# A six-stage decoder on one core: the last batch's front is laid beside the attentions

## The chip, the cores and the metric

The kernel runs on one core of one Trainium2 chip. A core has a matrix engine (TensorE, PE in the profile; the loading of its weights is shown apart as PEld), a vector engine (DVE), a scalar engine (ACT), a general engine that here issues gathers (POOL), and a queue engine that issues plain transfers (SP). Every engine takes its instructions strictly in the order of its own list, and waits at an instruction until the semaphores that it names have been raised by other engines or by transfers. The metric is the device time of one execution in microseconds (us), as the median of several runs.

## The reference

The input is `x` of 4 batches x 256 tokens x 256 channels, in float32. Six residual stages follow one another; each reads the layer-normalised sum so far:

```python
x = x + attn0(ln(x))      # gated linear attention: 16 heads, a decaying scan over the 256 tokens of a batch
x = x + experts4(ln(x))   # 4 experts chosen by token id; weights are the context itself
x = x + peer(ln(x))       # 8 heads x 8 of 2025 experts per token: gather 64 rows, weigh, add
x = x + local(ln(x))      # causal convolution (3 taps), 8-head attention within blocks of 16 tokens, projection
x = x + cross(ln(x), ctx) # 16-head attention of all 1024 tokens to all 1024 context rows, with int8-like rounding
x = x + moe(ln(x))        # top 2 of 16 experts, and a shared one
```

Three of them matter in detail. The denominator of the linear attention is one number per token and head:

```python
running_kv, running_ksum = scan(k * v, decay), scan(k, decay)
den = clip(sum(q * running_ksum, -1, keepdims=True), 1e-6)
out = (q * running_kv / den) @ w_out
```

The gathered experts of the third stage:

```python
z = einsum('btd,bthkd->bthk', h, down_embed[indices])     # 64 rows of 128 per token
z = silu(z * softmax(scores))
out = einsum('bthk,bthkd->btd', z, up_embed[indices])     # 64 rows of 256 per token
```

And the cross attention, where every query head sees all 1024 keys, so that a softmax row has 1024 elements:

```python
q, k, v = fake_quantised(x @ Wq + bq), fake_quantised(ctx @ Wk + bk), fake_quantised(ctx @ Wv + bv)
attn = softmax(q @ k.T); attn = round(attn / (max / 255)) * (max / 255)
out = (attn @ v) @ Wp + bp
```

## The kernel before

The 1024 tokens are eight tiles of 128 tokens (`xt[0]` to `xt[7]`, kept in SBUF throughout), two for each of four batches. Batch b has tiles 2b and 2b+1.

**Streams and the planner.** Everything up to the mixture of experts is written as Python generators, called streams. While the program is built, `Clock.weave` (L110) advances at each step the stream that can go on earliest by a rough clock. `Clock.note` (L80) prices each instruction, and a `yield` names the engine that comes next and, if need be, a condition. The order in which instructions are recorded becomes the fixed order of PE, ACT and DVE. Nothing is reordered on the chip: an instruction that is recorded early and not ready holds up all that stands behind it on its engine. Nearly all instructions are recorded through one helper, so that they carry line L76 in the profile and are told apart by their tiles.

**The fronts** (`front`, L348). A front is the first three stages up to the choice of the gathered experts for one batch (two tiles): normalisation, projections, scans, division by the denominator, four context experts, up and down projection, similarities, and top-k by MAX8 and FIND_INDEX8. Its outcome is `idxT[t]` and `pT[t]`, the row numbers and weights of a tile; from then on tile t is `known`. `follow` (L1122) starts front 2 when tile 1 is known and front 3 when tile 3 is known. The fronts use seven PSUM banks as one set of slots (`bank`, L346). An eighth bank, `accs`, holds the sums of the gathers and of the cross attention.

**The gathers** (`fetches`, L607, and `weigh`, L618). Each tile has eight chunks, 64 in all. For a chunk, SP issues two broadcast loads (`hb`), and POOL issues eight indirect gathers into one of three `g` buffers. DVE multiplies and reduces (`g`, `z`, `u`), ACT takes a tanh (`th`), DVE writes weights into `blk`, and PE adds eight matmuls into `accs`. The fetch of chunk n waits until chunk n-3 has been summed. After a tile's eighth chunk DVE adds `accs` to `xt[t]`; the tile is then `added`.

**The hand-over** (`turn`, L748). When all four fronts and the keys and values are done, the fronts' memory and banks are given up at once, the weights of the later stages are loaded into that memory, and PSUM is divided anew: two double banks `sc` for scores, one bank `tp`, two banks `mm`.

**Local attention, queries and units.** `locals_` (L940) takes the groups (0,1), (2,3), (4,5), (6), (7) one after another, each once its tiles are added. `local_attention` (L806) normalises, convolves, projects, attends within blocks, adds to `xt`, and then in the same generator normalises again, forms and rounds the queries and transposes them into `qT`. `units` (L947) are three streams that share 128 units, 16 heads for each of eight tiles. A unit is: two score matmuls into an `sc` slot, a maximum over 1024 scores (DVE), `nb` (DVE), an exponential to 8-bit `e` (ACT), two transposes into `tp` (PE), a cast `qqT` (ACT), and eight small matmuls into `accs`. After the 16th unit of a tile `cross_out` (L987) divides (`ao`) and projects; then `route` (L1032) normalises, chooses two of 16 experts and adds the shared one.

**The end.** Once tile 7 is added, the gathers' memory is given up and `weights` (L792) loads the experts' `w13`. After the last `route` the slots are worked out, and 31 tiles of routed rows run through `up` (L1200) and `down` (L1221); the results are gathered and written out.

Of the kernel before, what the change touches and what calls it, by code (L numbers as in the profile page):

```python
# [11 lines left out]
F32 = mybir.dt.float32  # L12
# [39 lines left out]
class Clock:  # L52
# [6 lines left out]
    def __init__(self, nc):  # L59
        self.free = dict.fromkeys(("tensor", "scalar", "vector", "gpsimd", "sync"), 0.0)  # L60
        self.t = self.end = 0.0
        self.last = None
        for name in self.free:
            setattr(self, name, self._Engine(self, name, getattr(nc, name)))
# [15 lines left out]
    def note(self, engine, op, out, args, kw):  # L80
        if engine == "sync":
            return
        n, late = math.prod(out.shape[1:]), 0.0
# [5 lines left out]
        elif engine == "scalar":  # L89
            scaled, summed = isinstance(kw.get("scale"), bass.AP), "accum_out" in kw  # L90
            cost, late = 0.06 + n * 0.00083 + 0.23 * (scaled or summed) + 0.06 * (scaled and summed), 0.1
        elif engine == "gpsimd":
            cost = 1.23
        elif op in ("max", "max_index", "tensor_reduce"):
            src = args[1] if op != "max_index" else args[2]
            cost = (0.195 if op == "tensor_reduce" else 0.16) + 0.00104 * math.prod(src.shape[1:])
        elif op == "reciprocal":
            cost = 0.1 + 0.0064 * n
        elif op == "tensor_tensor_scan":
            cost = 0.2 + 0.0022 * n  # L100
        else:
            cost = 0.195 + (0.00054 if op in ("tensor_scalar", "tensor_copy") else 0.00104) * n
        if self.last not in (None, engine):
            self.t = self.end + self.HOP
        start = max(self.free[engine], self.t)
        self.free[engine] = start + cost
        self.end = max(self.end, start + cost + late)
        self.last = engine

    def weave(self, streams):  # L110

# [3 lines left out]
        while live:  # L115
            able = []
            for s in live:
                t = s.t
                engine, wait = s.wait
                if isinstance(wait, Slots):  # L120
                    if not wait.left:
                        continue
                    t = max(t, wait.at)
                elif wait is not None:
                    at = wait()
                    if at is None:
                        continue
                    t = max(t, at)
                able.append((max(t, self.free[engine]), t, s))
            _, t, s = min(able, key=lambda x: (x[0] - x[2].lead, x[1]))  # L130
            self.lead = s.lead
# [7 lines left out]
            s.t = self.end + self.HOP  # L139

    def fork(self, *gens):

        made = [Stream(g, self.lead, self.end + self.HOP) for g in gens]
# [4 lines left out]
class Stream:  # L148
    def __init__(self, gen, lead=0.0, start=0.0):
        self.gen, self.lead, self.t, self.done = gen, lead, start, None  # L150
# [3 lines left out]
class Slots:  # L154
# [3 lines left out]
    def __init__(self, clock, pool, tag, n):  # L158
        self.clock, self.pool, self.tag, self.left, self.at = clock, pool, tag, n, 0.0
        self.n = n  # L160

    def take(self, shape, dtype=F32):
        while not self.left:
            yield "tensor", self
        self.left -= 1
        return self.pool.tile(shape, dtype, name=self.tag, tag=self.tag, bufs=self.n)

    def give(self):
        self.left += 1
        self.at = self.clock.end  # L170


def decoder(ctx, tc, a, out):
# [7 lines left out]
    front_ctx = ctx.enter_context(ExitStack())  # L181
    attend_ctx = ctx.enter_context(ExitStack())
    work_ctx = ctx.enter_context(ExitStack())
    A = SimpleNamespace(turned=None)
    wa = front_ctx.enter_context(tc.tile_pool(name="wa", bufs=1, side="right"))

# [29 lines left out]
    wkv = load(wa, "wkv", [P, 2, 2 * D], rows("wkv"))  # L216
    bk_b = load(wa, "bkb", [P, D], a["bkv"][:, 0:D].to_broadcast([P, D]))
    bv_c = load(base, "bv_c", [P, 2])
    for b in range(2, NB):
# [11 lines left out]
    headones = wa.tile([P, P // XD, XD], F32, name="headones", tag="headones")  # L231
    nc.gpsimd.memset(headones, 1.0)
    nc.gpsimd.affine_select(out=headones, in_=headones, compare_op=ALU.is_ge, fill=0.0, base=0,
                            pattern=[[-XD, P // XD], [0, XD]], channel_multiplier=1)
    nc.gpsimd.affine_select(out=headones, in_=headones, compare_op=ALU.is_ge, fill=0.0, base=XD - 1,
                            pattern=[[XD, P // XD], [0, XD]], channel_multiplier=-1)
# [28 lines left out]

    gather_ctx = ctx.enter_context(ExitStack())
    gather = gather_ctx.enter_context(tc.tile_pool(name="gather", bufs=3))
    fr = front_ctx.enter_context(tc.tile_pool(name="fr", bufs=1, side="right"))
    psum_ctx = ctx.enter_context(ExitStack())
    psp = psum_ctx.enter_context(tc.tile_pool(name="psp", bufs=1, space=PSUM))  # L270
    psf = front_ctx.enter_context(tc.tile_pool(name="psf", bufs=1, space=PSUM))
# [13 lines left out]
    def layernorm_T(pool, sfx, bank, tiles, dst, col0=0, store=None):  # L285
# [3 lines left out]
        for i, t in enumerate(tiles):  # L289
            st = pool.tile([P, 6], F32, name="ln_st", tag="ln_st" + sfx, bufs=2)  # L290
            ve_.bn_stats(st, xt[t])
            ve_.bn_aggr(mv[:, i, :], st)

        ve = pool.tile([P, n], F32, name="ln_ve", tag="ln_ve" + sfx)
        ve_.tensor_scalar(ve, mv[:, :, 1], EPS, None, ALU.add)
        half = pool.tile([P, n], I32, name="ln_half", tag="ln_half" + sfx)
        ve_.tensor_scalar(half, ve.bitcast(I32), 1, None, ALU.logical_shift_right)
        rstd = pool.tile([P, n], F32, name="ln_rstd", tag="ln_rstd" + sfx)
        ve_.tensor_scalar(rstd.bitcast(I32), half, -1.0, float(0x5F3759DF), ALU.mult, ALU.add)
        nt = pool.tile([P, n], F32, name="ln_nt", tag="ln_nt" + sfx)  # L300
        for _ in range(3):
            ve_.scalar_tensor_tensor(nt, rstd, -0.5, rstd, ALU.mult, ALU.mult)
            ve_.tensor_tensor(nt, nt, ve, ALU.mult)
            ve_.scalar_tensor_tensor(rstd, nt, 1.5, rstd, ALU.add, ALU.mult)
        nmr = pool.tile([P, n], F32, name="ln_nmr", tag="ln_nmr" + sfx)
# [3 lines left out]
        for i, t in enumerate(tiles):  # L309
            xn = pool.tile([P, D], F32, name="ln_xn", tag="ln_xn" + sfx, bufs=2)  # L310
# [9 lines left out]
        yield "scalar", None  # L320
        se_.copy(dst[:, :, col0:col0 + n * P].rearrange("p k (i q) -> p k i q", i=n), tp)
        bank.give()
# [21 lines left out]
    hdram, pT, idxT, known = {}, {}, {}, {}  # L344
    fronts_left = [NB]
    bank = Slots(ck, psf, "f", 7)  # L346

    def front(b):  # L348
        tiles = (2 * b, 2 * b + 1)
        o_ = str(b % 2)  # L350

# [8 lines left out]
        yield from layernorm_T(fr, o_, bank, tiles, xnT)  # L360
# [3 lines left out]
        def proj(j):  # L364
# [7 lines left out]
            if j == 2:  # L372
                yield "vector", lambda: made.get(1)
                ve_.tensor_tensor(kv, p, kf, ALU.mult)
                bank.give()
# [11 lines left out]
            bank.give()  # L387
# [9 lines left out]
        den = yield from bank.take([P, 2, N])  # L397
        for c in range(2):
            te_.matmul(den[:, c, :], headones.rearrange("p g j -> p (g j)"), rk[:, c, :], start=True, stop=True)
        ve_.tensor_tensor(kf, kf, qf, ALU.mult)  # L400
        yield "vector", None
        rden = t2([P, 2, N], "rden")
        ve_.tensor_scalar(rden, den, 1e-6, None, ALU.max)
        bank.give()
        ve_.reciprocal(rden, rden)
        ve_.tensor_tensor(kf, kf, rden, ALU.mult)
# [8 lines left out]
        bank.give()  # L415
# [4 lines left out]
        yield from layernorm_T(fr, o_, bank, tiles, xnT)  # L420

        def experts(*es):
            for e in es:
# [10 lines left out]
                bank.give()  # L434
# [11 lines left out]
                bank.give()  # L446
# [6 lines left out]
        yield from layernorm_T(fr, o_, bank, tiles, xnT)  # L453
        ups = {}

        def raise_(*gs):
            for g in gs:
# [10 lines left out]
                bank.give()  # L468
# [13 lines left out]
        bank.give()  # L482
# [8 lines left out]
        bank.give()  # L491
# [5 lines left out]
        def similar(s):  # L497
            qs = []
            for r in range(2):
# [7 lines left out]
                bank.give()  # L507
# [3 lines left out]
            for i in range(2):  # L511
# [6 lines left out]
                bank.give()  # L518
# [3 lines left out]
        def choose(i, t):  # L522
# [52 lines left out]
            for j, (dic, dt, nm) in enumerate(((idxT, I32, "idxT"), (pT, F32, "pT"))):  # L575
                d = gather.tile([P, 4, 16], dt, name=nm, tag=nm, bufs=8)
                for o in range(2):
                    half = slice(o * 64, o * 64 + 64)
                    se_.copy(d[half], tq[half, j, :, o, :])
                dic[t] = d  # L580
            bank.give()
# [4 lines left out]
        fronts_left[0] -= 1  # L586
# [31 lines left out]
    def weigh():  # L618

        for n in range(8 * NT):  # L620
# [10 lines left out]
            u = gather.tile([P, 4, 2], F32, name="u", tag="u")  # L631
            ve_.tensor_tensor(u, z, pT[t][:, :, i0:i0 + 2], ALU.mult)
            yield "scalar", None
            th = gather.tile([P, 4, 2], F32, name="th", tag="th")
# [3 lines left out]
            for o in range(2):  # L638
                half = slice(o * 64, o * 64 + 64)
                ve_.scalar_tensor_tensor(yb[half, :, :, 31 + 16 * o], th[half], 1.0, u[half], ALU.add, ALU.mult)  # L640
# [15 lines left out]
    k3 = fr.tile([P, 2 * XH, 4, XD], BF16, name="k3", tag="k3")  # L656
# [23 lines left out]
    def keys_values():  # L680
        for b in range(NB):
# [6 lines left out]
            k1 = fr.tile([P, 2, D], F32, name="k1", tag="k1")  # L688
            ve_.tensor_tensor(k1, pk_, bc(bk_b, 1, 2), ALU.add)
            bank.give()  # L690
            kv_, ks = quantise(fr, k1, 1.0, "k")
# [12 lines left out]
            for i in range(2):  # L704
# [6 lines left out]
                bank.give()  # L711
# [3 lines left out]
        for c in range(2):  # L715
            v1 = fr.tile([P, T], F32, name="v1", tag="v1")
            for n in range(2):
# [6 lines left out]
                bank.give()  # L724
# [3 lines left out]
            rv = fr.tile([P, 1], F32, name="rv", tag="rv", bufs=2)  # L728
# [4 lines left out]
            vb = fr.tile([P, T], BF16, name="vb", tag="vb")  # L733
# [9 lines left out]
            bank.give()  # L743
# [4 lines left out]
    def turn():  # L748
        yield "vector", lambda: None if fronts_left[0] or not kv_done else max(kv_done[0], *known.values())
        front_ctx.close()  # L750
        wb = attend_ctx.enter_context(tc.tile_pool(name="wb", bufs=1, side="right"))
# [11 lines left out]
        A.bq_b = load(wb, "bxq", [P, D], a["bxq"].to_broadcast([P, D]))  # L763
# [559 lines left out]
```

## Time and profile before

| | us |
|---|---|
| median of 3 runs | 1350.36 (1349.67 to 1356.5) |
| profiled execution | 1364.85 |
| its span, from the first instruction to the last | 1363.1 |
| PE, PEld busy | 865.9, 519.5 |
| DVE busy | 848.3 |
| ACT busy | 522.2 |
| POOL busy | 567.7 |

No engine is busy for more than 64% of the span. The kernel goes through stages with different limits, so the shares over the whole span say little; the numbers that matter are those of a stage. Times in the views are counted from the start of the span. In a row, "x64" is the number of instructions, the last column the time for which the engine stood idle just before them, with what ended the wait; "issue" means that no waiting on another engine is seen, and "remote" that the releaser isn't known.

### The profile page before, as it was taken

How to read it: one execution, taken by the hardware profiler on the slowest of the kernel's cores; microseconds unless marked ns; L12 is line 12 of the kernel's file. 1: busy time of each engine (PE TensorE's matmuls, PEld its weight loads, DVE VectorE, ACT ScalarE, POOL GpSimd, SP SyncE). 2: the span in 40 equal slices, each digit the busy share in tenths (PEclk: the TensorE clock that was granted, in tenths of full speed). 3: DMA queues.
4: the chain of work that ended last, by engine and by line, in shares of the span. 5: the costliest groups of instructions: out<-in, count | busy, mean ns of one | idle time of the engine just before them, and what ended most of it. 6: DMA issues, size and time to landing. Idle time of an engine off the chain costs nothing. (4 is left out here: it accounts for less than half of the span.)

```text
span 1363.1 us, 15375 instructions
## 1 busy us (share of the span) xinstructions
PE 865.9 (64%) x4869; PEld 519.5 (38%) x4869; DVE 848.3 (62%) x2369; ACT 522.2 (38%) x1053; POOL 567.7 (42%) x584
## 2 busy tenths in 40 slices
PE   4670679831353715456866479876777878748991
PEld 3560457620232503323433234433434544324550
DVE  5459797759963495455566676669676566642222
ACT  1241124410111301214464554565567767722220
POOL 1004666655464666755464654657600000003314
PEclk8795779965667856657566656777676556558995
DMA  5012567655654688756565754557723000012323
GB/s 184 1 36 74 148 144 171 168 156 141 150 141 123 174 228 247 164 143 163 115 154 149 153 166 129 161 156 175 157 87 124 1 9 1 4 27 74 86 70 104
DMA packets 93165, 165.56 MB, mean 121 GB/s; under 512 B 14858, under 2 KB 65275, under 8 KB 93084
## 3 DMA queue, kind: packets, MB, share of 16 engines
q0 software_dynamic: 35024, 106.86, 26.3%
q1 hardware_dynamic: 58060, 57.72, 20.8%
q8 instruction: 39, 0.64, 0.2%
q14 instruction: 42, 0.34, 0.1%
HBM read 157.85 MB, written 6.68 MB: 121 GB/s over the span
## 5 line engine op out<-in xcount | busy, mean ns | idle before, releaser
L76 POOL DMA_INDIRECT g<-in_table,idxT x512 | 516.7, 1009 | 465.5 <-PE accs L76 148.4
L76 DVE TENSOR_REDUCE mx<-sc 128x1 f32<-128x1024 f32 x128 | 156.0, 1219 | 101.3 <-PE sc L76 53.6
L76 ACT ACTIVATE e<-sc,nb,qs_q 128x1024 uint8<-128x1024 f32 x128 | 154.3, 1206 | 49.9 <-DVE nb L76 29.6
L76 ACT CAST qqT<-tp 128x1024 bf16<-128x1024 uint8 x128 | 129.4, 1011 | 103.4 <-PE tp L76 51.1
L76 PE MATMUL accs<-g,blk 128*32 128x256 f32 x1024 | 100.4, 518 | 83.8 <-DVE blk L76 40.0
L1205 POOL DMA_INDIRECT xr<-xs,smap x31 | 29.4, 947 | 297.5 <-DVE smap L1192 240.3
L76 PE MATMUL sc<-kT,qT 64*128 64x512 bf16 x256 | 115.1, 547 | 33.6 <-ACT e L76 17.4
L76 PE MATMUL tp<-ident,e 128*128 128x128 f32 x256 | 77.3, 397 | 76.1 <-ACT qqT L76 71.5
L76 PEld LDWEIGHTS tp<-ident,e 128*128 128x128 f32 x256 | 35.3, 186 | 146.2 <-ACT qqT L76 97.9
L76 DVE TENSOR_TENSOR g<-g,hb 128x1024 f32<-128x1024 f32 x64 | 78.3, 1224 | 12.1 <-issue 7.1
L76 PEld LDWEIGHTS accs<-g,blk 128*32 128x32 f32 x1024 | 33.5, 137 | 130.7 <-issue 63.6
L76 DVE TENSOR_REDUCE z<-g 128x8 f32<-128x1024 f32 x64 | 78.1, 1220 | 2.2
L76 PEld LDWEIGHTS <-qqT 128*128 128x128 bf16 x1024 | 44.8, 106 | 58.9 <-ACT qqT L76 26.1
L76 ACT ACTIVATE ln_xn<-x,ln_nmr,ln_rstd 128x256 f32<-128x256 f32 x48 | 26.6, 594 | 90.6 <-DVE ln_nmr L76 72.8
L76 PE MATMUL accs<-vi,qqT 128*128 128x16 bf16 x1024 | 48.3, 176 | 19.3 <-ACT qqT L76 10.3
L76 ACT ACTIVATE th<-u 128x8 f32<-128x8 f32 x64 | 13.5, 211 | 108.2 <-DVE u L76 74.0
L1218 DVE TENSOR_TENSOR hd<-hd,ph 128x176 f32<-128x176 f32 x31 | 10.4, 338 | 63.0 <-ACT hd L1217 63.0
L1214 PE MATMUL ph<-w,xrT 128*128 x124 | 48.9, 507 | 0.8 <-DVE xrT L1211 0.7
L76 PE MATMUL f<-ident,ix 128*128 128x128 f32 x8 | 3.6, 447 | 66.1 <-DVE sm L76 66.1
L76 PE MATMUL f<-w_ctxT,aT 128*128 128x256 f32 x128 | 32.5, 406 | 18.4 <-DVE aT L76 17.3
L76 DVE TENSOR_SCALAR nb<-mx,nsq,ln 128x1 f32<-128x1 f32 x128 | 34.9, 273 | 7.5 <-ACT e L76 0.5
L76 PEld LDWEIGHTS <-qT 64*128 64x128 bf16 x256 | 18.2, 102 | 55.4 <-issue 46.1
(290 smaller groups left out, 1725.5 us busy)
## 6 DMA issues: line engine op xcount, KB each, us to landing
hb<-hdram SPq DMA_DIRECT2D x128, 256.0 KB
g<-in_table,idxT POOLq DMA_INDIRECT x512
w<-in_w SPq DMA_DIRECT2D x16, 352.0 KB
ys<-yr SPq DMA_DIRECT2D x31, 128.0 KB
w_w2a<-in_w SPq DMA_DIRECT2D x1, 2048.0 KB
x<-in_x SPq DMA_DIRECT2D x8, 128.0 KB
w_ctxT<-in_ctxT SPq DMA_DIRECT2D x1, 1024.0 KB
w_w_up<-in_w_up SPq DMA_DIRECT2D x1, 1024.0 KB
```

The lines of the kernel that those rows point to most:

```text
L76: return emit(*args, **kw)
L1205: nc.gpsimd.indirect_dma_start(out=xr, out_offset=None, in_=xs, in_offset=bass.IndirectOffsetOnAxis(ap=smap[:, i:i + 1], axis=0))
L1214: nc.tensor.matmul(ph.rearrange("p j n -> p (j n)"), xrT[:, k, :], w13[:, bass.ds(e, 1), k, :], start=(k == 0), stop=(k == 1))
L1218: nc.vector.tensor_tensor(hd, hd, ph[:, 1, :], ALU.mult)
```

## The change

- **Memory in three steps.** Fronts 0 and 2 work in a pool of their own (with the keys and values), fronts 1 and 3 in another. `turn` gives up the first pool when fronts 0 and 2 and the keys and values are done, loads the weights of local attention and queries, and opens the attentions' work pool. A new stream `free` gives up the second pool once all fronts are done, and loads the rest (`wp`, the router's and the shared expert's weights, `w2a`, and `w2b`, which had been loaded after the last `route`). The gathers' memory follows last, as before.
- **PSUM shared by all.** `Banks` takes the place of `Slots`: seven banks as single ones at first, and from `turn` on two pairs and three single ones. The pairs are for scores alone. The three single banks serve whatever asks: front 3, local attention, queries, the units' transposes, the output and the routing.
- **By tile.** `local_attention(t)` takes one tile, its second part as two halves of four heads; `queries(t)` is a stream of its own. Eight local attentions and eight query stages take the place of five groups. The buffers of `qT` fall from four to two, those of `qqT` from three to two, and at most two units may stand between their transposes and their sums. The key bias is added on DVE and no longer on ACT.
- **Denominator.** It is formed as 16 numbers per token, inverted, transposed and spread over the channels by a matmul, instead of being spread first and inverted at 512 elements per lane.
- **Gathers.** `pT` has the halves of a token apart, with zeros, so that one DVE instruction writes `blk` where two did.
- **The planner.** `Clock.note` follows which tile each operand was made in, prices DVE's small instructions lower, and breaks ties by a rank. The normalisation yields after each small instruction.

```diff
-        yield "vector", lambda: None if fronts_left[0] or not kv_done else max(kv_done[0], *known.values())
-        front_ctx.close()
+        yield "vector", lambda: None if 0 in fronts_left or 2 in fronts_left or not kv_done else max(kv_done[0], known[5])
+        bank.closing = True
+        yield "vector", lambda: None if bank.held else 0.0
+        banks(2, 2, 1, 1, 1)
+        even_ctx.close()
...
+    def free():
+        yield "vector", lambda: None if fronts_left or A.turned is None else max(A.turned, *known.values())
+        front_ctx.close()
...
+        A.w2a = load(w2, "w2a", [P, NE, D], a["w2"][:, 0:P, :].rearrange("e p n -> p e n"))
+        A.w2b = load(w2, "w2b", [EH, NE, D], a["w2"][:, P:EI, :].rearrange("e p n -> p e n"))
+        A.work2 = work_ctx.enter_context(tc.tile_pool(name="work2", bufs=1))
+        A.freed = ck.end
...
-    def local_attention(*tiles):
+    def local_attention(t):
-        n = len(tiles)
-        W, c0 = n * P, tiles[0] % 2 * P
...
+        for part, lo in ((0, 0), (1, AW)):
+            p = yield from bank.take([P, 4, P])
+            for m in range(4):
+                te_.matmul(p[:, m, :], A.wqk[lo:lo + AW, m * P:(m + 1) * P], qk[lo:lo + AW, :], start=True, stop=True)
...
+                ve_.tensor_tensor(kh, p, bc(A.bk, 2, P), ALU.add)
...
+        yield from ck.fork(half(0), half(1))
...
+        local[t] = ck.end
...
+    def queries(t):
+        yield from layernorm_T(work, "q", (t,), xnTq)
...
+        yield "tensor", lambda: 0.0 if t < QB else summed.get(("x", t - QB))
+        tp = yield from bank.take([P, 8, P], BF16)
...
     def units(k, n):
-            psc = yield from A.sc.take([P, T])
+            psc = yield from bank.take([P, T], n=2)
...
-            tp = yield from A.tp.take([P, 2, P])
+            yield "tensor", lambda: None if weighted[0] == 2 else 0.0 if t == 0 else summed.get(("o", t - 1))
+            weighted[0] += 1
+            tp = yield from bank.take([P, 2, P])
...
-            qqT = work.tile([P, 8, P], BF16, name="qqT", tag="qqT", bufs=3)
+            qqT = work.tile([P, 8, P], BF16, name="qqT", tag="qqT", bufs=2)
...
     def front(b):
-        den = yield from bank.take([P, 2, N])
-        for c in range(2):
-            te_.matmul(den[:, c, :], headones.rearrange("p g j -> p (g j)"), rk[:, c, :], start=True, stop=True)
+        den = yield from bank.take([P, 2, XH])
+        for i in range(2):
+            for c in range(2):
+                te_.matmul(den[:, i, 8 * c:8 * c + 8], rk[:, c, i * P:(i + 1) * P], headones, start=True, stop=True)
...
     def weigh():
-            for o in range(2):
-                half = slice(o * 64, o * 64 + 64)
-                ve_.scalar_tensor_tensor(yb[half, :, :, 31 + 16 * o], th[half], 1.0, u[half], ALU.add, ALU.mult)
+            ve_.scalar_tensor_tensor(yb[:, :, :, 31:63:16], th, 1.0, u, ALU.add, ALU.mult)
...
-        ck.weave([*[Stream(follow(b), (3.0, 0.0, 0.0, 0.0)[b], (0.0, 20.0, 0.0, 0.0)[b]) for b in range(NB)],
-                  Stream(keys_values(), 0.0, 25.0), Stream(fetches(), 20.0), Stream(weigh()), Stream(turn()),
-                  Stream(weights()), Stream(locals_()), *[Stream(after_turn(units, k, 3)) for k in range(3)],
+        ck.weave([*[Stream(follow(b), (3.0, 0.0, 0.0, 0.0)[b], (0.0, 20.0, 0.0, 0.0)[b], (0, 0, 1, 1)[b]) for b in range(NB)],
+                  Stream(keys_values(), 0.0, 25.0, 1), Stream(fetches(), 20.0), Stream(weigh(), rank=0), Stream(turn()), Stream(free()),
+                  Stream(weights()), Stream(locals_()), Stream(all_queries(), rank=0), *[Stream(after_turn(units, k, 3)) for k in range(3)],
```

`Banks`, the new slots:

```python
def find(self, n):
    if self.closing:
        return None
    sets = self.pairs if n == 2 else [(k,) for k in self.free if k >= self.single]
    sets = [(max(self.free[k] for k in ks), ks) for ks in sets if all(k in self.free for k in ks)]
    return min(sets) if sets else None

def give(self, v):
    for k in self.held.pop(id(v))[1]:
        self.free[k] = self.clock.end + self.clock.HOP
```

## The prediction

> **What bounds the kernel now.** I read the slices of the page first, then a table by stage, then single tiles to date the stages, then the waits of the stages.
>
> ```profile
> PE   4670679831353715456866479876777878748991
> DVE  5459797759963495455566676669676566642222
> ACT  1241124410111301214464554565567767722220
> POOL 1004666655464666755464654657600000003314
> ```
>
> A slice is 34.1 us. The reader sees POOL's gathers from slice 4 to slice 29, DVE nearly full while fronts run (to slice 10), a dip of all three engines in slices 11 to 17, then PE and ACT filling up, and a last stretch without POOL.
>
> ```profile
> L76 ACT CAST idxT<-f x16: 189/206/208, 117.7 to 517.4; 64x64 int32<-64x64 f32 x16
> L76 ACT COPY qT<-mm x5: 994/1012/1017, 607.7 to 1143.8; 128x1024 bf16<-128x1024 bf16 x5
> L76 DVE TENSOR_TENSOR x<-accs,x x8: 414/425/426, 247.5 to 1017.9; 128x256 f32<-128x256 f32 x8
> L76 DVE TENSOR_TENSOR ao<-accs,sums x8: 424/425/425, 706.5 to 1200.0; 128x256 f32<-128x256 f32 x8
> ```
>
> The last two columns of times date the stages (first and last start): the last front ends at 517.4, the first queries are ready at 607.7, tile 7's gathers are added at 1017.9, its cross attention is divided at 1200.0. By stage (busy us of PE, PEld, DVE, ACT, POOL with instruction counts, then granted clock, share of the transfers, GB/s):
>
> ```profile
> 137.00:377.00 240.00, 139.98 (x775) 98.61 (x773) 191.05 (x629) 59.04 (x126) 141.98 (x138) 0.75 0.62 153
> 377.00:517.00 140.00, 64.28 (x363) 42.41 (x363) 84.23 (x289) 21.58 (x55) 83.23 (x83) 0.68 0.67 171
> 517.00:608.00 91.00, 47.01 (x281) 29.12 (x280) 45.31 (x104) 19.85 (x66) 56.83 (x58) 0.65 0.74 188
> 608.00:1018.00 410.00, 294.82 (x1926) 155.79 (x1926) 274.54 (x563) 225.38 (x414) 220.31 (x221) 0.65 0.58 145
> 1018.00:1200.00 182.00, 141.91 (x835) 79.12 (x834) 113.96 (x272) 132.51 (x224) 0.00 (x0) 0.58 0.10 33
> ```
>
> From 377 to 608 front 3 runs alone beside the gathers, and then the first local attention: 231 us in which DVE is busy for 130, PE for 111, ACT for 41. The 128 units begin only then. When the gathers end at 1018, 49 units are left over (DVE's order has 79 before tile 7's addition), so 182 us follow in which the gathers are not the bound. The last 163 us (routing's end, experts, output) hang on PE's expert matmuls and are not touched.
>
> ```profile
> POOL g L76 <- PE accs L76: 60.8, 12, 14.3
> DVE mx L76 <- remote: 33.6, 8, 8.3
> ACT qqT L76 <- remote: 31.9, 8, 9.9
> ```
>
> These are waits of 608 to 1018 (us, times, longest). Eight back-to-back gathers take 10.04 us, but chunk 34 to chunk 63 take 13.76 us each (DVE's multiplies start at 607 and 1006): POOL waits for a `g` buffer, because a landed chunk waits its turn in DVE's order for 15 to 25 us. The pace belongs to the interleaved order, not to one full engine.
>
> **The change, part by part.** The changed program's orders were read beside the trace.
>
> *The fronts up to chunk 24.* Four reciprocals of 3.35 us become small ones (0.25, the 16-element row) with a transpose and a spreading matmul: DVE -12.4. The second `blk` write goes: 24 x 0.166 = -4.0. Against that, tile 0's local attention and queries (about 16 us of DVE by rows) now stand before chunk 24, and 16 of front 3's MAX8/FIND_INDEX8 groups (0.189 + 0.092 + 0.199 each, 7.7) behind it. The sum is about -8. This stretch has DVE at 80% from 137 to 377, so I take -7: chunk 24 starts at 473, not 480. If none counts it is 0; if PE's and ACT's new steps in the front's chain (two transposes at 0.39, a copy at 0.37, two matmuls at 0.53) stay uncovered, about +2 per front, +8.
>
> *Units begin earlier.* `turn` now stands behind chunk 18, the first units behind chunk 25 instead of chunk 34. The weights for it are loaded on SP at chunk 8, behind the release of the keys' memory at chunk 6; `w_wp` and `w2a` stand on SP behind front 3's end at chunk 31, ahead of chunk 34's `hb`, which waits for chunk 31's buffer anyway. No load blocks a chunk that is not blocked already. `w2b` was issued at 1219.5 and first read at 1243; loading it early gains nothing. By tile 7's addition 97 units are done instead of 79.
>
> *What it costs the gathers.* DVE's list from chunk 24 to tile 7's addition holds 354 us now (measured, 480 to 1018). After: 18 more units (1.219 + 0.273) = +27; front 3's part +8; six key biases at 0.69 = +4; more normalisations, masks and queries by tile, less the merged `blk`, +13. That is 406. POOL's floor for 40 chunks is 402. Two bounds for the pace: as in chunks 48 to 63 (12.9 us), where DVE was densest (147 us in 812 to 1018, 72%), or DVE at the whole stretch's share (354/538 = 66%), which gives 617 us. I take 13.76, the pace with units beside: chunks 34 to 48, with less DVE work, were not faster than 48 to 63, so the pace doesn't follow DVE's content. Then chunk 63 starts at 473 + 39 x 13.76 = 1010, tile 7 is added at 1021 (now 1018). Bounds 988 and 1090.
>
> *The stretch after the gathers.* In the new order tile 5's last unit comes at once (3 us). Then stand 14 units, tile 7's local attention and queries, and the route of tiles 4 and 5: nearly what stands now between tile 5's division (1083.7) and tile 6's (1150.7), with 16 units: 67 us. Its floor is the chain alone: by rows, normalisation 5, convolution 5, projections 5, scores to probabilities 12, products 6, queries 14, so 47; its ceiling what tile 7 takes now from its convolution to `qT` (1066.6 to 1143.8) and a normalisation, 86. Then 16 units and route 6: now 14 of them take 49.3 us (1150.7 to 1200.0), so 56; floor 16 x 2.42 (ACT's 1.206 + 0.198 + 1.011) = 39. Together 126 (89 to 145) instead of 182.
>
> *Shared banks.* Now a unit's transposes wait for the single `tp` bank: 34.2 us on PEld in the last stretch ("PEld tp <- ACT qqT"). With three shared banks a part may go. I cost it at 0; with all of it gone for 31 of 49 units, -22. Planner prices and ranks: 0, inside the pace's bounds.
>
> *The sum.* 1021 + 126 + 163 = 1310 of span instead of 1363.1, from +3 and -56. The profiled execution took 1364.85, 1.75 over its span, and the median of the runs is 0.9894 of that: (1310 + 1.75) x 0.9894 = 1298.
>
> [...] The granted clock is 0.58 in the last stretch (PE busy 78%) and 0.94 with the experts (91%). [...]
>
> **Rivals.**
>
> *DVE becomes the bound (slower).* If DVE can be kept busy only as now, 66%, the 406 us take 617, tile 7 is added at 1090, and 1090 + 126 + 163 = 1379 gives 1366. For it: chunks wait for DVE's turn already. Against it: 80% from 137 to 377, 72% in the last half of the gathers. It turns the sign where DVE's share is under 406/(1018 + 56 - 473) = 68%.
>
> *The attentions do not really start earlier.* Front 3 had seven banks and now shares three with local attention and transposes; if it and tile 0 hold each other up, units begin at 600 as now, the left-over is 49 units again, and only the 7 us of the fronts remain: 1356, so 1343. Against it: tile 6 is needed at chunk 48, and its indices stand at chunk 29, 19 chunks or 260 us ahead. [...]
>
> *Faster than the sum.* The pace is 12.9, so tile 7 is added at 988, and the wait for `tp` goes (-22): 988 + 104 + 163 = 1255, so 1243. For it: the stalls by "remote" and the 98 us of PEld's waits for `tp` lie in the order and the banks. Against it: they are spread over 590 us, and the new order has two units in flight at most.
>
> **How the numbers follow.** The sum has 0.55 (its own range 1275 to 1325), DVE as bound 0.14, no earlier start 0.09, faster than the sum 0.22. The range 1245 to 1355 leaves out the slow rival and the lower part of the fast one. A measurement here can tell about 0.5% from no change, 1343.6 to 1357.1. Faster by more: 0.55 + 0.22 + 0.03 = 0.80; within: 0.06; slower: 0.14.
>
> **What would show it.** In the profile after: first `qT` near 490; tile 7's addition at 988 to 1040 (1090 means DVE); last `ao` 110 to 145 behind it; DVE over 70% between chunk 24 and that addition; the rest, 163, unchanged. I am wrong if chunks take over 15 us, or if the stretch behind the gathers stays over 165.

## The result, and the profile after

Beside four runs of the kernel before (median 1351.63 us) the changed kernel took 1300.31 us (four runs, 1296.12 to 1306.98): ratio 0.9612, 95% interval 0.9577 to 0.9647. The profiled execution took 1306.98 us, with a span of 1305.3.

The slices of the changed kernel's page (32.6 us each), for comparison with those shown of before:

```profile
PE   4672489355735686757777776675687787749991
DVE  4569587684478458986677757665676677542222
ACT  1241034112202143544756636554456587712220
POOL 2003665655456546666555755544544000003214
```

The dip of all three engines in slices 11 to 17 has shrunk to single slices: from slice 15 to slice 35, PE and DVE show 5 to 9 tenths throughout.

Single tiles of the changed kernel (last columns: first and last start, us):

```profile
L77 ACT CAST idxT<-bank x16: 205/206/207, 113.1 to 580.7; 64x64 int32<-64x64 f32 x16
L77 DVE TENSOR_TENSOR x<-accs,x x8: 405/424/425, 247.1 to 1027.4; 128x256 f32<-128x256 f32 x8
L77 DVE TENSOR_TENSOR ao<-accs,sums x8: 424/425/425, 597.3 to 1142.6; 128x256 f32<-128x256 f32 x8
```

The last front ends at 580.7 (before: 517.4), the first unit's scores start at 502 (before: near 609), tile 7 is added at 1027.4 (before: 1017.9), and its cross attention is divided at 1142.6 (before: 1200.0). By stage (busy us of PE, PEld, DVE, ACT, POOL with counts, granted clock, share of the transfers, GB/s; chunk 0 to chunk 24, to tile 7's addition, to its division, to the end):

```profile
135.00:485.00 350.00, 218.76 (x1167) 153.89 (x1168) 226.97 (x757) 83.43 (x198) 199.07 (x196) 0.75 0.60 152
485.00:1027.50 542.50, 374.65 (x2588) 209.22 (x2587) 384.69 (x986) 286.70 (x549) 300.80 (x302) 0.66 0.59 155
1027.50:1142.60 115.10, 89.07 (x566) 49.84 (x564) 76.62 (x206) 85.57 (x146) 0.00 (x0) 0.66 0.16 54
1142.60:1305.30 162.70, 110.33 (x413) 61.45 (x413) 50.59 (x182) 30.77 (x104) 44.39 (x47) 0.80 0.25 71
```

The same cuts through the kernel before give 343, 538, 182 and 163 us. So chunk 24 starts 5 us later than before, tile 7's addition comes 10 us later, and then the stretch behind the gathers is 67 us shorter. All of the gain stands there. (Of one variant below, `oldden_b`, two of four runs were over 1.5% slower than the fastest and are left out of its ratio; its profile is of one of these.) Waits in that stretch of the changed kernel (us, times, longest):

```profile
PEld bank L77 <- ACT e L77: 20.2, 15, 4.7
DVE mx L77 <- PE bank L77: 20.0, 13, 4.2
PE bank L77 <- ACT e L77: 15.8, 15, 3.8
PEld L77 <- ACT qqT L77: 12.8, 17, 2.3
```

In the kernel before, the transposes waited there for the `tp` bank, until `qqT` had been read out of it:

```profile
PEld tp L76 <- ACT qqT L76: 34.2, 25, 2.9
```

Now they wait for `e`, their input.

### The profile page after: what moved, and what is told of

Its sections match the earlier page's. It is cut to its first block, busy times and chain, and to the rows that moved or that the text cites. A ratio compares the mean times of both kernels' runs of the same rounds, so it can differ in the third digit from the quotient of the medians.

```text
span 1305.3 us, 15780 instructions
## 1 busy us (share of the span) xinstructions
PE 865.8 (66%) x5029; PEld 531.6 (41%) x5029; DVE 825.5 (63%) x2457; ACT 519.0 (40%) x1060; POOL 569.0 (44%) x595
## 4 chain that ended last, share of the span: by engine, by line
PE 42%; DVE 24%; ACT 11%; another core or an unknown queue 9%; issue 7%; DMA 5%; POOL 2%; SPq 1%; DVEq 0%; POOLq 0%; ACTq 0%
PE bank L77 28%; PE accs L77 6%; DVE mx L77 5%; PE ph L1313 3%; ACT qqT L77 3%; ACT e L77 3%; DMA g<-in_table,idxT 3%; DVE g L77 2%; DVE z L77 2%; POOL g L77 2%; PE py L1330 1%; DVE oh L77 1%; PE py L1329 1%; DVE mi L77 1%
## 5 line engine op out<-in xcount | busy, mean ns | idle before, releaser
L77 DVE TENSOR_REDUCE mx<-bank 128x1 f32<-128x1024 f32 x128 | 155.8, 1217 | 85.9 <-PE bank L77 55.6
L77 ACT ACTIVATE e<-bank,nb,qs_q 128x1024 uint8<-128x1024 f32 x128 | 154.2, 1205 | 51.1 <-DVE nb L77 29.8
L77 ACT CAST qqT<-bank 128x1024 bf16<-128x1024 uint8 x128 | 127.6, 1010 | 116.0 <-PE bank L77 57.3
L77 PE MATMUL bank<-kT,qT 64*128 64x512 bf16 x256 | 102.3, 508 | 22.2 <-ACT e L77 10.5
L77 PE MATMUL bank<-ident,e 128*128 128x128 f32 x256 | 72.5, 388 | 39.3 <-ACT e L77 15.6
L77 DVE TENSOR_REDUCE z<-g 128x8 f32<-128x1024 f32 x64 | 78.1, 1220 | 2.2
L77 PEld LDWEIGHTS bank<-ident,e 128*128 128x128 f32 x256 | 35.9, 185 | 91.3 <-issue 42.3
L77 ACT ACTIVATE th<-u 128x16 f32<-128x16 f32 x64 | 14.0, 218 | 91.3 <-DVE u L77 64.1
L77 PE MATMUL bank<-ident,ln_xn 128*128 128x128 f32 x96 | 25.0, 379 | 37.5 <-ACT ln_xn L77 21.2
L77 PE MATMUL bank<-xnT,w_w_up 128*128 128x256 f32 x128 | 37.1, 452 | 4.9 <-issue 2.8
L77 DVE SCALAR_TENSOR_TENSOR blk<-th,u 128x16 f32<-128x16 f32 x64 | 11.4, 177 | 41.9 <-ACT th L77 36.1
```

Source lines behind the costliest of these rows:

```text
L77: return emit(*args, **kw)
```

## The experiments

The variants ran on three chips, four kernels on each, always beside the kernel before: chip B (before 1239.98), chip C (1368.39) and chip D (1351.84). Times are compared on one chip only. The changed kernel ran again on C and on D:

> The kernel before, unchanged, for a profile on the chip on which the variants ran (there it takes 1240, not 1351). Theory: the stretches without gathers (from tile 7's addition on: 182 and 163 us) are as long as on the first chip, and the 110 us that are missing come out of the waits for a releaser that isn't known, which the variants' profiles don't have. Rival: the first chip was slower in the engines or the gathers themselves; then single durations differ (gather 946 ns, reduction 1217 ns, cast 1010 ns on the first).

> The changed kernel, unchanged, beside the kernel before on the variants' chip. Theory: the same 31 units are left behind tile 7's addition, so the last stretch is 115 +- 4 as on the first chip, and the gain is about the same in us, 45 to 55 (time 1185 to 1195); the reduction more on DVE (1198) then cost 3 to 13 us, much less than its 49, and the early start (held back: 1197) is worth 2 to 12. Rival (where the waits without a known releaser are gone, DVE has 88% of the stretch ahead of tile 7's addition and is the bound there): the added reduction cost nearly its 49 us, so the time is 1150 to 1165.

> The changed kernel, unchanged, as the measure for the three others of this call. Theory (the gain lies behind the last gather and hangs on no chip): ratio 0.96 to the kernel before, whatever time that takes here, and 112 to 119 us from tile 7's addition to the last division.

| chip | kernel | us | ratio to before, interval |
|---|---|---|---|
| C | changed | 1312.13 | 0.9622 (0.9554 to 0.9690) |
| D | changed | 1293.71 | 0.9564 (0.9508 to 0.9620) |

Which chip the first comparison ran on is not known; its ratio was 0.9612. The gain is about the same in all three comparisons, and the stretch behind the addition is 118.5 and 115.1 us, inside what was expected of it (111 to 119, and 112 to 119). The chip that the first two expectations speak of is B, but `before_b` and `after_b` ran on C, so these two say nothing about B. `before_b` took 1361.81, and its profile repeats the first one: chunk 24 at 476.4, tile 7's addition at 1015.5, last division at 1196.9. Chip B never ran the changed kernel; what this leaves open is said at each run.

**The early start held back.**

```diff
-        yield "vector", lambda: None if 0 in fronts_left or 2 in fronts_left or not kv_done else max(kv_done[0], known[5])
+        yield "vector", lambda: None if fronts_left or not kv_done else max(kv_done[0], *known.values())
```

> The changed kernel, but `turn` waits for all four fronts, so the first units stand behind chunk 32 and 89 of them (not 97) ahead of tile 7's addition. Theory (the gain is units moved ahead of the last gather): 39 units are left instead of 31, at the 3.71 us per unit that the last stretch shows in both kernels (182/49 and 115/31), so about +30: span 1335, time 1330; first qT near 590, last stretch near 145, chunk 24 to chunk 63 as fast as now or a little faster. Rival (the gain comes from the shared banks, the division by tile and the smaller denominators, and the early start is worth little): within 10 us of the changed kernel's 1300.

> `turn` held until all four fronts are done, again, now beside the changed kernel: 89 units ahead of tile 7's addition, 39 left. Theory (the gain is the units that are moved ahead): last stretch longer by 8 x 2 to 8 x 3.7, so +16 to +30; the chunks from 24 to 63, with eight units less beside them, up to 10 us faster; together +8 to +25 against the changed kernel. Rival (banks, tiles and small denominators carry the gain): -5 to +5.

On chip D: 1315.64 us, ratio 0.9755 (0.9671 to 0.9840), 22 us more than the changed kernel, inside the theory's 8 to 25, and 36 less than the kernel before. By stage:

```profile
133.90:478.10 344.20, 209.04 (x1108) 145.83 (x1108) 221.92 (x756) 79.40 (x178) 201.79 (x198) 0.74 0.62 156
478.10:1017.00 538.90, 377.34 (x2527) 218.86 (x2528) 374.56 (x945) 272.38 (x540) 302.44 (x300) 0.66 0.59 156
1017.00:1149.60 132.60, 102.82 (x687) 59.79 (x685) 93.67 (x249) 105.52 (x174) 0.00 (x0) 0.67 0.14 47
```

(The changed kernel there: 345.5, 537.2 and 115.1.) The addition stands at 1017, as in the changed kernel; the eight units cost 17.5 us behind it, 2.2 each, and nothing ahead of it. So the early start is worth about 20 us of the gain. The larger rest is there without it, as the rival had it for the whole. With `turn` waiting for what it waited for before, 89 units and not 79 stand ahead of the addition: the division by tile lets the queries of tile 0 follow its own local attention and no longer that of the pair (0,1); the shared banks and the planner's new prices are in this too, and the run doesn't tell them apart; no run undoes the division by tile or the planner's prices alone. And the 39 units behind take 3.4 us each, where those of before took 3.7. On chip B the held-back kernel took 1197.24 (ratio 0.9663); the times that its expectation names can't be compared with that, but its stretch behind the addition, 131.7, is shorter than the 145 expected at 3.7 us a unit.

**One bank for the transposes.** Of the three shared banks one is kept for the units' transposes, two for all else.

```diff
-        sets = self.pairs if n == 2 else [(k,) for k in self.free if k >= self.single]
+        sets = self.pairs if n == 2 else [(k,) for k in self.free if k >= self.single and (not self.single or (k == 6) == (n == 3))]
...
-            tp = yield from bank.take([P, 2, P])
+            tp = yield from bank.take([P, 2, P], n=3)
```

> The changed kernel, but of the three shared banks one is kept for the units' transposes alone and the other two for all else, as in the kernel before. 91 units stand ahead of tile 7's addition, not 97. Theory (sharing the banks is worth little by itself): 37 units are left, at 3.7 to 3.9 us each 137 to 144 instead of 115, so +22 to +29 behind the addition, and the chunks ahead of it as fast or a few us faster: +15 to +29. Rival (the shared banks carry the gain): +35 to +45, close to the kernel before.

On chip C: 1339.82 us, ratio 0.9833 (0.9758 to 0.9908), 28 us more than the changed kernel, inside the theory's 15 to 29 and at its end. Windows from chunk 24 to the addition and from there to the last division, and the first wait of the latter:

```profile
478.20:1031.70 553.50, 378.35 (x2534) 216.08 (x2533) 379.14 (x982) 278.74 (x535) 302.87 (x301) 0.65 0.61 153
1031.70:1170.00 138.30, 104.78 (x642) 58.02 (x639) 85.92 (x220) 97.63 (x162) 0.00 (x0) 0.61 0.13 44
```

```profile
PEld bank L77 <- ACT qqT L77: 28.7, 18, 3.1
```

The wait of the kernel before is back; in the changed kernel on the same chip it is 1.5 us. The addition comes 7.5 us later than in `after_b`, and the stretch behind it is 20 us longer: by `hold_b`'s 2.2 us, measured on another chip, the six units account for 13 of these, and the other 7 are put down to the bank itself. This split is an estimate. Sharing then acts twice: it lets the planner place units earlier, and it takes a wait out of many units.

**More units ahead of the last gathers.** Three settings of one number, the planner's guess of when a chunk has landed (8 us in the kernel): 5; 24; and 17 from chunk 44 on alone.

```diff
-            landed[n] = ck.end + LANDS
+            landed[n] = ck.end + (8.0 if n < 44 else 17.0)
```

> The changed kernel with the planner's landing time at 17 us instead of 8 from chunk 44 on: the order is the same up to there, and then 104 instead of 97 units stand ahead of tile 7's addition, 24 behind it. Theory (units ahead of the addition cost the gathers little, but behind it tile 7's own chain has a floor): the stretch behind falls from about 115 to 97 to 112, since local attention and queries of tile 7 (47 to 67) and its 16 units (39 to 56) remain; the addition comes 0 to 15 us later; together -15 to +10. Rival (every unit ahead is free and every unit behind costs 3.7): -26. Rival (each unit costs the chunks what it saves behind): +5 to +20.

> The changed kernel with one number of the planner changed: it takes a chunk's gathers to land 24 us after their issue, not 8, and so writes more of the fronts and the attentions ahead of each chunk: 112 units stand ahead of tile 7's addition, and only tile 7's own 16 behind it. Theory (units ahead of the last gather are free as long as the chunks don't slow): the last stretch falls from 115 to what tile 7 needs alone, its local attention and queries 47 to 67 and its units 39 to 56, so 86 to 115; but each chunk waits longer for its turn on DVE, and three buffers turn that into pace: chunk 24 to 63 from 13.7 to 14 to 15.5 us each, so tile 7's addition 10 to 70 later. Together -15 to +60, more likely slower. Rival (chunks wait in DVE's order for nothing, the gathers have room): tile 7's addition stays near 1027, time -10 to -29.

> The changed kernel with the planner's landing time of a chunk at 5 us, not 8, so that the chunks stand earlier in DVE's order against fronts and units; 95 units ahead of tile 7's addition, not 97. Theory (each chunk's latency from issue to sum over three buffers sets the pace): chunks 24 to 63 are faster by 0 to 0.5 us each, so tile 7's addition 0 to 20 us earlier, and the two units more behind it cost 7: -13 to +7. Rival (DVE's work ahead of the addition sets the pace, whatever the order): tile 7's addition moves by the 2 x 1.5 us of the units alone, time +4.

| chip | kernel | units ahead | us | ratio to before, interval |
|---|---|---|---|---|
| D | 17 from chunk 44 | 104 | 1315.97 | 0.9766 (0.9696 to 0.9837) |
| B | 24 throughout | 112 | 1301.21 | 1.0497 (1.0480 to 1.0515) |
| C | 5 throughout | 95 | 1341.70 | 0.9810 (0.9737 to 0.9883) |

The first is the cleanest, since its order is that of the changed kernel up to chunk 44. It is 22 us slower than the changed kernel: the theory (-15 to +10) missed it, and it lies just past the rival by which each unit costs the chunks what it saves behind (+5 to +20). Its stages:

```profile
487.00:1050.60 563.60, 395.89 (x2677) 220.29 (x2677) 400.00 (x1022) 304.68 (x574) 302.66 (x301) 0.65 0.59 150
1050.60:1151.10 100.50, 78.03 (x476) 41.72 (x475) 62.93 (x170) 69.25 (x121) 0.00 (x0) 0.65 0.18 59
```

Behind the addition it saves 14.6 us with seven units less, as the theory had it (97 to 112). But the addition comes 33 us later. About 5 of these were there when the orders part, near 751 us in the changed kernel, and so don't come from the changed order. The rest follows: chunks 40 to 48 take 128.6 us instead of 115.0, and 48 to 63 take 214.7 instead of 201.7. The waits of the chunks' buffers from 600 us to the addition (451 and 417 us), first in `late17`, then in the changed kernel on the same chip:

```profile
POOL g L77 <- PE accs L77: 105.5, 14, 18.7
```

```profile
POOL g L77 <- PE accs L77: 83.0, 16, 9.3
```

These waits grew by 22.5 us, which fits this account: a chunk that stands behind more units in DVE's order is summed later, and the buffer it holds keeps a gather waiting. With 24 throughout the stretch behind is 89.8 us (forecast 86 to 115), but the fronts are written ahead of the chunks too: chunk 24 starts at 514.8, against 420.4 on that chip with the changed kernel's fronts (`dve_more`), and the total lies far outside the expectation (119 us over `oldden`, below, on that chip). With 5, chunks 24 to 63 take 14.39 us each and not less than 13.76: both theories missed it. Between 493 and 503 us all engines but POOL stand still there (shown in the last section), and front 3 ends 42 us later than in `after_b`. What made the chunks slower beyond that one standstill is open.

**DVE's work ahead of the addition.** One reduction more per chunk, order unchanged, its result overwritten.

```diff
+            if n >= 24:
+                nc.vector.tensor_reduce(z, gd, AX.X, ALU.max)
             ve_.tensor_reduce(z, gd, AX.X, ALU.add)
```

> The changed kernel, order unchanged, with one reduction more on DVE (128x1024, 1.22 us) in each of chunks 24 to 63, its result overwritten: 40 x 1.22 = 49 us more DVE work ahead of tile 7's addition, DVE from 71% to about 78% of that stretch. Theory (the pace is the chunk's latency over three buffers, DVE has gaps left): a third of it to a half, so tile 7's addition 16 to 25 us later and the time +16 to +25. Rival (DVE is the bound at the share it has now): +49.

On chip B: 1198.36 us, ratio 0.9671 (0.9654 to 0.9687). `dve_more`, then `oldden` (below), which has nearly the changed kernel's units and came without the extra work, from chunk 24 to the addition:

```profile
420.50:914.80 494.30, 360.29 (x2588) 201.63 (x2587) 430.58 (x1025) 289.27 (x549) 308.52 (x304) 0.68 0.67 172
```

```profile
422.90:894.40 471.50, 357.17 (x2621) 203.90 (x2620) 384.04 (x1002) 287.98 (x553) 307.78 (x302) 0.72 0.71 180
```

46.5 us more of DVE work lengthen the stretch by 22.8, half of it, as the theory had it, and DVE reaches 87%. Against `oldden`, of another order and 95 units, this is an indication; the changed kernel itself did not run there. What the run does show: with 49 us of DVE work added, the kernel is still 3.3% faster than before on that chip, with DVE at a share far above the 66% that the slow rival took as a limit.

**The denominators of before** in the changed kernel: spread first, then a reciprocal over 512 elements.

```diff
-        den = yield from bank.take([P, 2, XH])
...
+        den = yield from bank.take([P, 2, N])
+        for c in range(2):
+            te_.matmul(den[:, c, :], headones.rearrange("p g j -> p (g j)"), rk[:, c, :], start=True, stop=True)
```

> The changed kernel with the denominators of before (spread first, reciprocal over 512 elements). Theory of the forecast (DVE work saved in the fronts counts): chunk 24 starts 7 to 12 us later than its 485, time +5 to +12. Rival (the new transpose, copy and spreading matmul stand in the front's own chain and cost what DVE saves, which is why chunk 24 came at 485 and not at 473): chunk 24 at 473 to 485, time -12 to 0. The order shifts a little too: 95 units, not 97, ahead of tile 7's addition, which by itself is +7.

> The denominators of before in the changed kernel, again, now beside it: 95 units ahead of tile 7's addition. Theory of the forecast (12.4 us of DVE work saved in the fronts): +5 to +15. Rival (the longer chain of the new denominators, transpose, copy and spreading matmul, costs what DVE saves): -10 to +3.

On chip D the ratio is 0.9526 (0.9431 to 0.9620), on chip B 0.9539 (1182.23 us). By the ratios it lies 5 us under the changed kernel on chip D, inside the rival's -10 to +3, but the intervals overlap, so the two are not told apart. The stretch from chunk 0 to chunk 24, on chip D with old and with new denominators:

```profile
133.80:464.70 330.90, 197.34 (x1081) 137.96 (x1081) 230.81 (x740) 78.28 (x185) 200.90 (x195) 0.76 0.64 160
```

```profile
134.60:480.10 345.50, 215.14 (x1169) 151.57 (x1170) 227.27 (x757) 83.82 (x199) 199.15 (x196) 0.75 0.61 154
```

With the new ones DVE is busy for 3.5 us less there, and PE for 18 us more. That is not the saving itself, since the planner's order shifts: three of the four denominators stand in the stretch (the first, at 25 us, stands ahead of chunk 0), and by their rows each saves 3.5 us (3.35 and 0.69 us for reciprocal and clip become 0.35 and 0.19), 10.5 in all, while other work moved in ahead of chunk 24. The stretch is 15 us longer on chip D, by one profile of each; on chip B it is 3.5 us shorter (287.3 in `dve_more`, whose order is the changed kernel's, 290.8 in `oldden`). So of the saved DVE work 3.5 us at most are found as time, and whether the longer chain costs something is open.

## Why the prediction was right, and where it was not

| | forecast | measured |
|---|---|---|
| first `qT` | 490 | 501.1 |
| chunk 24 starts | 473 | 485.0 |
| chunk 24 to 63, each | 13.76 | 13.73 |
| tile 7 added | 1021 | 1027.4 |
| to the last division | 126 (89 to 145) | 115.1 |
| the rest | 163 | 162.7 |
| span | 1310 | 1305.3 |
| time (median) | 1298 | 1300.31 |

*The main step held: more units ahead of the last gather, at no price in the pace.* On chip C, at chunk 48, the kernel before has 38 units done at 807.0 us, the changed kernel 54 at 809.9. Those 16 units went into time in which the engines had stood idle, for chunk 48 comes only 3 us later. Between chunks 48 and 63 both do about 40 units. 97 units instead of 79 stand ahead of the addition, and the stretch behind shrinks by 67 us.

*Mis-attributed: where the units come from.* The rival "the attentions do not really start earlier" was priced at 1343, only 7 us of gain. `hold_b` is that case in its outcome (first scores at 581 us), and it keeps 36 of 58 us on chip D. The step that failed is "the left-over is 49 units again": 39 are left over, because the rest of the change brings ten units ahead, and those behind are cheaper. The sum put all 18 units down to the early start; eight of them are.

*Mis-sized: shared banks, "I cost it at 0" (bounds 0 and -22).* The transposes' waits for `qqT` are all but gone from the stretch behind (34.2 us on PEld before, 0.8 now), and it came out 11 us under the sum: by the divisions of tiles 5, 6 and 7 its parts are 7, 58 and 50 us, where the forecast had 3, 67 and 56. `onetp` prices the sharing at 28 us in all on its chip, most of it, by the estimate above, through the order. Three shared banks did not hold up front 3 beside tile 0 in a way that counts: its last indices come 63 us later than before, at 581, and tile 6's gathers start only at 767. With a bank kept for the transposes, as in the kernel before, 28.7 us of waits return in `onetp`; with the shared three they are 1.5 us on the same chip.

*Wrong: the fronts, "I take -7".* DVE's busy time from chunk 0 to chunk 24 fell by 14 us (241.2 to 227.0), more than forecast, and chunk 24 came 5 us later (4 on chip C). The forecast had the small reciprocal at 0.25 us and left the clip out; by the rows above the four denominators save DVE 14.0 us and not 12.4. The inference failed that DVE at 80% makes its saved work the path's saved time: DVE's share simply fell, and chunk 24 lay within the bound named for an uncovered chain, +8. Holding `turn` back gives 2 of them back (478.1 against 480.1); the rest is not settled.

*Right for the pace, by luck in its parts.* 13.73 is a mean of 12.5 (chunks 24 to 34), 13.7 and 14.6 (48 to 63; 13.8 and 13.5 on C and D). DVE as the bound (1366) was out: its share is 71%, over the 68% that the rival needed to fall, and 385 us of work, not 406; the terms beyond the 18 units were counted 21 us too high. But "the pace doesn't follow DVE's content" is not general: `late17` shows that units pushed in front of late chunks delay them by as much as they save or more.

*The clock.* The granted clock behind the addition is 0.66, 0.59 and 0.66 in three profiles of the changed kernel, and the stretch 115.1, 118.5 and 115.1 us; before it was 0.58 and 0.59. Between these profiles the stretch differs by 3.4 us. PE is busy for 77% of the stretch in the profiles at 0.66, for 82% in the one at 0.59, and for 78 and 77% before. The clock differs between profiles of one kernel in one order, so no run here shows what sets it, or what the change gained by it.

*The sum's nearness is partly chance:* chunk 24 came 12 us later than forecast and the stretch behind the addition was 11 us shorter, which nearly cancel. The span came 5 us below the forecast, and the median stands at 0.9949 of the profiled execution instead of the 0.9894 taken over from before, which gives 7 us back. `lands5` and `late17` show how far another order of the same work can lie from the changed kernel: 30 and 22 us.

## What to carry to other kernels

In a pipeline with a long middle of transfers, count how much dependent work is done when the last transfer lands; what is left then is the gain or the loss. Moving work ahead paid here where engines stood idle in the middle (16 units more by chunk 48, which came 3 us later), and not where units delayed a transfer's buffer (`late17`: 22.5 us more of waits for buffers, 22 us slower). Busy time saved on an engine at 80% need not be time saved: here DVE had 14 us less to do in a stretch that became 7 us longer. And undo one part at a time: the part with the plainest name (the early start) carried little more than a third of the gain.

## What the runs showed of the hardware

The same kernel runs much faster on one chip, and nearly all of the difference lies where gathers run. The held-back kernel took 1315.64 us on chip D and 1197.24 on chip B. Its first two stages on chip B (its third was 131.7):

```profile
132.30:424.30 292.00, 194.80 (x1108) 137.90 (x1108) 221.04 (x756) 80.00 (x178) 199.30 (x196) 0.79 0.74 182
424.30:899.20 474.90, 340.38 (x2527) 198.60 (x2528) 370.85 (x944) 271.90 (x540) 304.15 (x302) 0.72 0.69 178
```

116 of 118 us come from these two (344.2 and 538.9 on chip D); behind the last addition 132.6 and 131.7 us, and the rest, 163.7 and 163.9, are equal. Single gathers and reductions take the same time (a gather 949 and 946 ns in the median, a reduction 1220 and 1220). What differs are waits whose releaser the trace doesn't know: 145 us of them in the list of all engines on chip D (two engines can wait at once, so this is no share of the span), none on chip B. They show in the first two profiles as well (178 us before, 202 after). The long ones are of DVE and ACT instructions that read what PE has just written (on chip D up to 13.4 us, before `kT`, and 10.7 us, before `x`). PE differs too: in these two stages it is busy for 209 and 377 us on chip D at a granted clock of 0.74 and 0.66, and for 195 and 340 us on chip B at 0.79 and 0.72. No run tells whether that is a cause of the difference or follows from the waits. In the timeline of `lands5` on chip C (start, us, engine, instruction, idle before):

```profile
489.81 1.24 PE L77 MATMUL bank<-up,w_w_down 128*128 128x256 f32 x5
492.93 0.44 PE L77 MATMUL bank<-ident,ln_xn 128*128 128x128 f32 x2 [0.25 <-issue]
503.03 0.48 DVE L77 TENSOR_SCALAR hT<-bank,w_b_down 128x256 f32<-128x256 f32 x1 [11.12 <-remote]
503.13 0.37 ACT L77 COPY xnTq<-bank 128x256 f32<-128x256 f32 x1 [10.25 <-remote]
```

Two engines that read what these two matmul groups wrote go on together at 503 us, though the trace has the groups as finished at 491 and 493. What held them for 12 and 10 us no run here tells, nor why such waits stand in none of the four profiles on chip B, and in none of six on C and D from 1020 us on.

In the three profiles of the changed kernel, chunk 24 to tile 7's addition takes 542.5, 543.8 and 537.2 us, and holds 2588 instructions of PE, 549 of ACT and 986, 986 and 985 of DVE, which agrees with a fixed order on each engine.
